# Moving layer 0's image resize and the weight preparation of layers 0 and 1 to the head of a four-layer convolution kernel

## The chip, the cores and the metric

The kernel runs on one core of a Trainium2 chip. A core has five instruction streams that run side by side and wait for one another through semaphores: TensorE (PE, with its weight loads shown apart as PEld), VectorE (DVE), ScalarE (ACT), GpSimd (POOL) and SyncE (SP), which here issues transfers only. Each stream runs its instructions in order. The metric is the device time of one execution, in microseconds.

## The reference

The input x has the shape (2, 64, 256, 256) in float32. Four layers follow, each of the form x = x + f(norm(x)), where norm is a group norm with 32 groups of two channels. A group norm needs the sums over the whole of x before the first element can be normalised.

```python
# layer 0
rimg = jax.image.resize(img, (b, 3, 256, 256), method='bilinear')    # from 512 x 512
rimg = jnp.einsum('oc,bchw->bohw', w_img, rimg)
em = jnp.concatenate([rimg, pos_embd], axis=1)        # pos_embd: w_pos times sines and cosines
feature_score = jnp.einsum('bckhw,bchw->bkhw', unfold3x3(em), em)    # dilation 2
comp_score = jax.nn.sigmoid(jnp.einsum('bckhw,c->bkhw', unfold3x3(inp), w_comp))
out = jnp.einsum('bckhw,bkhw->bchw', unfold3x3(inp), comp_score * feature_score)
```

Layer 1 is two Mamba blocks (a projection, a causal convolution of four taps, a scan over 65536 positions with 16 states, an output projection), each with a layer norm. Layer 2 is a projection to 384 channels, a filter in the Fourier domain of 8 x 8 patches, a 3 x 3 depthwise convolution, a gate and a projection back. Layer 3 is a quantised 8 x 8 cosine transform.

## The kernel before

The two images of the batch and their 64 channels fill the 128 partitions, and the 65536 pixels lie along the free axis. Everything is float32. Each layer reads its input from DRAM, writes its output to DRAM (y0, y1, y2, then out), and gathers the statistics of its output on the way; at its end `group_norm` makes the scale and shift ("coeffs", the tiles gns and gnb) for the next layer.

The order at the head of the program is this. `input_stats` (line 194) loads x in 16 tiles of 4096 columns (xin, three buffers) through SP, and DVE runs one bn_stats over each 512 columns, 128 in all (line 203). `group_norm` (bn_aggr at line 159, two small matmuls, a power on POOL at line 175, gnb at line 177) makes the coefficients.

`layer0` then calls `resize`. It loads the resize matrix rt and, for each of six images, loads src (line 218), multiplies it by rt in 32 matmuls (line 223), copies the four results from PSUM on ACT (mid, line 226), multiplies again in 16 matmuls (line 231), copies two results on DVE (dst, line 234) and stores them to the scratch tensor rimg in DRAM (line 235). src, mid, dst and the PSUM tile rps have two buffers each. After that `layer0` loads its own weights (pos, w_comp, w_e, w_y), makes wcomp and by_row, fills 32 partitions of the two tiles rts with the positions (line 274), and has POOL zero the frames gs and es and eleven tiles called moved (line 288). The memory of these tiles partly follows on that of `resize`.

Layer 0 itself is a pipeline of 128 steps of two image rows. A step normalises x (fea, line 191), makes the embedding e and the gated feature g (`embed`, lines 319 to 334), multiplies e by its shifted neighbours on POOL (pr, line 356), sums over channels on PE (pf, line 361), and puts the parts together (lines 366 to 440). Its order on every engine is written out by hand, between the lines `with tc.manual_schedule(...)`. Outside of such blocks a scheduler places the instructions of each engine: roughly in program order, but an instruction whose inputs are ready may be put ahead of one that must wait.

`layer1` first calls `mamba_weights` twice, for p1 and p2. Each call issues 26 small loads (helpers `load`, `load2` and `load_turned`, lines 134, 142 and 453, and lines 470 and 503) into temporary tiles, and rearranges them on DVE, ACT and PE into the kept tiles res, conv, dt, bc, a, d and out. The temporaries of p2 take the memory of those of p1. Ten further loads bring the layer norms' factors, sel and quad. Only then does `load(0)` (line 578) bring the first input tile x1t, and ACT normalises it into xin (line 191). The loop of layer 1 runs over 256 tasks (two blocks by 128 chunks of 512 positions), each in eight groups; its time is DVE's scan (line 792) and products.

All loads and stores of this kernel are issued by SP.

Of the kernel before, what the change touches and what calls it, by code (L numbers as in the profile page):

```python
# [10 lines left out]
F32 = mybir.dt.float32  # L11
# [3 lines left out]
PSUM = bass.MemoryType.PSUM  # L15
DRAM = bass.MemoryType.DRAM

P = 128
C = 64
# [101 lines left out]
class Kernel:  # L121
    def __init__(self, ctx, tc, a, out):
        self.tc, self.nc, self.a, self.out = tc, tc.nc, a, out
        self.const = ctx.enter_context(tc.tile_pool(name="const", bufs=1))
        self.dram = ctx.enter_context(tc.tile_pool(name="dram", bufs=1, space=DRAM))
        self.ident = self.load("c_ident")
        self.pair = self.load("c_pair")
        self.block = self.load("c_block")


    def load(self, name, pool=None):
        ap = self.a[name]
        t = (pool or self.const).tile(list(ap.shape), F32, name=f"t_{name}", tag=f"t_{name}")
        self.nc.sync.dma_start(t, ap)
        return t

    def load2(self, name, pool):

        ap = self.a[name]
        t = pool.tile([P, ap.shape[1]], F32, name=f"t_{name}", tag=f"t_{name}")  # L140
        for b in range(2):
            self.nc.sync.dma_start(t[b * C : (b + 1) * C], ap)
        return t

    def scratch(self, name, shape=(P, HW)):
# [45 lines left out]
        self.nc.scalar.activation(out, in_, AF.Identity, scale=coeffs[0], bias=coeffs[1])  # L191


    def input_stats(self, x):
        nc = self.nc
        stats = self.new_stats("stats_x")
        n = 4096
        with self.tc.tile_pool(name="in", bufs=3) as pool:
            for i in range(HW // n):
                t = pool.tile([P, n], F32, name="xin")  # L200
                nc.sync.dma_start(t, x[:, i * n : (i + 1) * n])
                for j in range(n // SUB):
                    nc.vector.bn_stats(
                        stats[:, i * (n // SUB) + j, :], t[:, j * SUB : (j + 1) * SUB]
                    )
        return self.group_norm("l0", stats, NSUB)


    def resize(self, rimg):
        nc, a = self.nc, self.a  # L210
        with self.tc.tile_pool(name="rs", bufs=2) as pool, self.tc.tile_pool(
            name="rsp", bufs=2, space=PSUM
        ) as psum:
            rt = pool.tile([P, 4, 256], F32, name="rt", bufs=1)
            nc.sync.dma_start(rt, a["c_resize"].rearrange("(k p) n -> p k n", p=P))
            for i in range(6):
                src = pool.tile([P, 4, 512], F32, name="src")
                nc.sync.dma_start(src, a["img"][i].rearrange("(k p) w -> p k w", p=P))
                mid = pool.tile([P, 4, 256], F32, name="mid")
                for wt in range(4):  # L220
                    ps = psum.tile([P, 256], F32, name="rps")
                    for k in range(4):
                        nc.tensor.matmul(
                            ps, src[:, k, wt * P : (wt + 1) * P], rt[:, k], start=k == 0, stop=k == 3
                        )
                    nc.scalar.copy(mid[:, wt], ps)
                dst = pool.tile([P, 2, 256], F32, name="dst")
                for ht in range(2):
                    ps = psum.tile([P, 256], F32, name="rps")
                    for k in range(4):  # L230
                        nc.tensor.matmul(
                            ps, mid[:, k, ht * P : (ht + 1) * P], rt[:, k], start=k == 0, stop=k == 3
                        )
                    nc.vector.tensor_copy(dst[:, ht], ps)
                nc.sync.dma_start(rimg[i].rearrange("(k p w) -> p k w", p=P, w=W), dst)

    def layer0(self, x, y, coeffs):

        nc, tc, a = self.nc, self.tc, self.a
        R = 8
        rimg = self.scratch("rimg", (6, HW))
        self.resize(rimg)
        stats = self.new_stats("stats_0")
        xv = x.rearrange("p (h w) -> p h w", w=W)
        yv = y.rearrange("p (h w) -> p h w", w=W)
        rv = rimg.rearrange("p (h w) -> p h w", w=W)
        nblk, per, nstep = H // R, R // 2, H // 2
        with ExitStack() as ctx:  # L250
            keep = ctx.enter_context(tc.tile_pool(name="l0k", bufs=1))
            pool = ctx.enter_context(tc.tile_pool(name="l0", bufs=2))

            pos = self.load("c_pos", keep)
            wc = self.load2("w_comp", keep)
# [3 lines left out]
            w_e = keep.tile([38, P], F32, name="w_e")  # L259
            w_y = keep.tile([32, P], F32, name="w_y")  # L260
            for t in (w_e, w_y):
                nc.vector.memset(t, 0.0)
            for b in range(2):
                nc.sync.dma_start(w_e[32 + 3 * b : 35 + 3 * b, C * b : C * b + 32], a["w_imgT"])
                nc.sync.dma_start(w_e[0:32, C * b + 32 : C * b + C], a["w_posT"][0:32])
                nc.sync.dma_start(w_y[:, C * b + 32 : C * b + C], a["w_posT"][32:64])
            by_row = keep.tile([P, H], F32, name="by_row")
            with tc.tile_pool(name="l0pr", bufs=1, space=PSUM) as psum:
                ps = psum.tile([P, H], F32, name="rowps")
# [109 lines left out]
            def add(eng, n, name, other):  # L379
                t = term[n, name]  # L380
                eng.tensor_add(t, t, other)

            load(0)
            load(1)
            E = mybir.EngineType
            with tc.manual_schedule(engines={E.PE, E.DVE, E.Activation, E.Pool, E.SP}):
                features(0)
                for t in range(nstep + 5):
# [6 lines left out]
                    n, last = t - 3, t - 4  # L395
# [21 lines left out]
                    if 0 <= n < nstep:  # L417
                        g, _, j = at(n)
# [16 lines left out]
                    if acc is not None:  # L435
                        k, s = divmod(last, per)
# [11 lines left out]
    def load_turned(self, name, pool):  # L448

        ap = self.a[name]  # L450
        t = pool.tile(list(ap.shape), F32, name=f"t_{name}", tag=f"t_{name}")
        for i in range(4):
            self.nc.sync.dma_start(t[i::4], ap[32 * i : 32 * i + 32])
        return t

    def mamba_weights(self, m, keep):
        nc, a = self.nc, self.a
        w = {}
        with self.tc.tile_pool(name=f"mw{m}", bufs=1) as pool, self.tc.tile_pool(
            name=f"mwp{m}", bufs=1, space=PSUM  # L460
        ) as psum:

            def kept(name, shape, dt=F32):
                return keep.tile(shape, dt, name=f"{m}{name}", tag=f"{m}{name}")
# [5 lines left out]
            nc.sync.dma_start(taps, a[f"{m}conv_wT"].partition_broadcast(P))  # L470
            w["conv"] = kept("conv", [P, 4, P])

            def turned(t):
# [14 lines left out]
            ps = psum.tile([P, P], F32, name=f"{m}ps")  # L488
# [11 lines left out]
                nc.vector.tensor_copy(w["bc"][:, j::8], bc[:, 5 - j : DS : 4])  # L500
            alog = pool.tile([P, 4, 4], F32, name=f"{m}alog")
            for q in range(4):
                nc.sync.dma_start(
                    alog[32 * q : 32 * q + 32],
                    a[f"{m}Alog"].rearrange("(i d) (q j) -> q d i j", d=32, j=4)[q],
                )
# [17 lines left out]
    def softplus(self, out, in_, bias):  # L524
        self.nc.scalar.activation(out, in_, AF.Softplus, bias=bias)

    def layer1(self, x, y, coeffs):
        nc, tc, a = self.nc, self.tc, self.a
        T = SUB
        nch = HW // T  # L530
        stats = self.new_stats("stats_1")
        with ExitStack() as ctx:
            keep = ctx.enter_context(tc.tile_pool(name="l1k", bufs=1))
            ws = [self.mamba_weights(m, keep) for m in ("p1_", "p2_")]
            mean = keep.tile([P, P], F32, name="mean")
            nc.scalar.mul(mean, self.block, 1.0 / C)
            lns = [(self.load2(f"ln{i}_g", keep), self.load2(f"ln{i}_b", keep)) for i in (1, 2)]
            sel = self.load("c_sel", keep).rearrange("k (b j p) -> k b j p", b=2, p=P)
            quad = self.load("c_quad", keep)
            eps = keep.tile([P, 1], F32, name="eps")  # L540
            nc.vector.memset(eps, 1e-5)
# [193 lines left out]
            with tc.manual_schedule(engines={E.PE, E.DVE, E.Activation, E.Pool, E.SP}):  # L735
# [29 lines left out]
                for g, (n, b, j) in enumerate(groups):  # L765
# [4 lines left out]
                    t, m = ts[n], tasks[n][0]  # L770
# [504 lines left out]
                nc.sync.dma_start(yv[:, rows], yt)  # L1275

    def run(self):
        x = self.a["x"]
        coeffs = self.input_stats(x)
        layers = (self.layer0, self.layer1, self.layer2, self.layer3)  # L1280
        for i, layer in enumerate(layers):
            y = self.out if i == 3 else self.scratch(f"y{i}")
            coeffs = layer(x, y, coeffs)
            x = y


@with_exitstack
# [52 lines left out]
```

## Time and profile before

| what | value |
|---|---|
| median of 3 runs | 19426.9 us (19423.29 to 19428.31) |
| the profiled execution | 19425.37 us |
| its span, first to last instruction | 19423.1 us |
| mean granted TensorE clock | 0.756 of full speed |
| DVE busy in the span | 17991.3 us, 93% |
| POOL busy | 16845.3 us, 87% |
| PE busy | 14534.9 us, 75% |
| ACT busy | 12151.6 us, 63% |
| costliest group | DVE scan, line 792, 8192 of 1262 ns |
| waits of SP's queue in `input_stats` for DVE | 58.9 us in 13 waits, longest 4.8 |

A row of the timeline gives the start in us, the time in us (of the whole group, where several like instructions are merged), the engine, the line, the operation with the tile it writes and those it reads, and in brackets the idle time before it and what ended it. SPq rows are the issuing of transfers, not the transfers themselves. The windows give the busy time of each engine within a stretch, and beside it the share of time in which the 16 DMA engines were at work.

### The profile page before, as it was taken

What the parts mean: (1) busy time and instruction counts of PE and PEld (TensorE: products, weight loads), DVE (VectorE), ACT (ScalarE), POOL (GpSimd) and SP (SyncE); (2) the same over time, 40 slices, a digit from 0 to 9 for tenths busy, and PEclk for the clock granted to TensorE, in tenths of its full rate; (3) what the DMA queues carried; (4) which work ended last, traced back from release to release, by engine and by line L of the source; (5) the groups of instructions that cost most, each with busy time, mean ns of one, the idle gap of its engine ahead of it and who ended that gap; (6) DMA issues with size and microseconds to landing.
All of it is one profiled execution on the core that took longest, in us unless ns stands there. A gap on an engine that the chain in (4) does not pass through costs nothing. (4 is left out here: it accounts for less than half of the span.)

```text
span 19423.1 us, 164029 instructions
## 1 busy us (share of the span) xinstructions
PE 14534.9 (75%) x48720; PEld 4763.2 (25%) x48720; DVE 17991.3 (93%) x15870; ACT 12151.6 (63%) x17418; POOL 16845.3 (87%) x8646
## 2 busy tenths in 40 slices
PE   7996677767777677676677677767777679999996
PEld 3441111111111111111111111111111134444444
DVE  6888999999999999999999999999999978888896
ACT  2325666666666666666666666666666657777774
POOL 5997888888888888888888888888888878888885
PEclk9996666666666666667666666666666679999997
DMA  3116666666666666666666666666666621111104
GB/s 122 57 50 150 149 156 152 150 155 149 155 150 151 156 151 152 150 150 155 152 151 154 149 156 150 150 156 151 152 150 151 154 52 32 32 32 31 32 29 147
DMA packets 662191, 2438.92 MB, mean 126 GB/s; under 512 B 131888, under 2 KB 201264, under 8 KB 450160
## 3 DMA queue, kind: packets, MB, share of 16 engines
q1 hardware_dynamic: 661296, 2428.43, 52.1%
q8 instruction: 385, 6.31, 0.1%
q14 instruction: 510, 4.18, 0.1%
HBM read 1990.14 MB, written 437.78 MB: 125 GB/s over the span
## 5 line engine op out<-in xcount | busy, mean ns | idle before, releaser
L792 DVE TENSOR_TENSOR_SCAN h<-da,st,h 128x512 f32<-128x512 f32 x8192 | 9837.9, 1262 | 310.0 <-ACT da L789 225.5
L796 POOL TENSOR_TENSOR h<-h,cb 128x2048 f32<-128x2048 f32 x2048 | 9252.4, 4518 | 164.7 <-POOL st L795 0.2
L789 ACT ACTIVATE da<-dl,p_a 128x512 f32<-128x512 f32 x8192 | 5564.3, 688 | 3976.2 <-DVE h L792 3884.3
L561 PE MATMUL py<-h,t_c_quad 128*32 128x512 f32 x16384 | 3250.7, 817 | 1649.2 <-POOL h L796 1648.3
L561 PE MATMUL pb<-bc,t_c_sel 64*128 64x512 f32 x3072 | 2696.1, 972 | 2386.6 <-DVE h L773 2381.3
L773 DVE TENSOR_TENSOR h<-dv,pb 128x2048 f32<-128x2048 f32 x1536 | 3471.5, 2260 | 40.8 <-DMA dv<-d_dv 40.8
L1023 POOL TENSOR_TENSOR gl<-gl,prod 128x512 f32<-128x512 f32 x2056 | 2606.1, 1272 | 460.9 <-ACT prod L1019 346.7
L755 POOL TENSOR_TENSOR h<-dv,cb 128x2048 f32<-128x2048 f32 x512 | 2318.7, 4529 | 16.7 <-DMA dl<-d_dl 16.7
L982 DVE SCALAR_TENSOR_TENSOR acc<-z,tap_b,acc 128x1024 f32<-128x1024 f32 (+1 forms) x1496 | 1901.6, 1271 | 22.3
L561 PEld LDWEIGHTS pb<-bc,t_c_sel 64*128 64x128 f32 x3072 | 660.9, 267 | 4410.5 <-DVE h L773 4347.0
L1019 ACT ACTIVATE prod<-z,tap_a 128x512 f32<-128x512 f32 x2056 | 1422.3, 716 | 284.8 <-POOL gl L1023 273.8
L795 POOL COPY st<-h 128x4 f32<-128x4 f32 x2048 | 383.5, 187 | 1362.9 <-DVE h L792 1331.9
L1079 PE MATMUL pcv<-z,diag 128*128 128x512 f32 x2322 | 1236.4, 642 | 179.9 <-ACT gl L1087 166.0
L561 PEld LDWEIGHTS py<-h,t_c_quad 128*32 128x32 f32 x16384 | 423.2, 122 | 3814.4 <-POOL h L796 3222.6
L561 PE MATMUL mm<-xin,p_conv 64*128 64x512 f32 x4096 | 1318.7, 773 | 15.1 <-DMA x1t<-y 15.1
L943 PE MATMUL pz<-t_c_inv,gf 128*128 128x128 f32 (+1 forms) x8192 | 964.7, 293 | 7.6 <-ACT z L951 7.3
L561 PE MATMUL mm<-u,p_dt 128*128 128x512 f32 x1024 | 929.1, 1061 | 0.0
L943 PEld LDWEIGHTS pz<-t_c_inv,gf 128*128 128x128 f32 (+1 forms) x8192 | 792.8, 170 | 484.2 <-issue 302.5
L924 DVE TENSOR_TENSOR gf<-feff,f 128x384 f32<-128x384 f32 x1024 | 558.7, 547 | 299.9 <-PE f L915 297.4
L561 PE MATMUL py<-u,p_d 128*128 128x512 f32 x1024 | 820.9, 895 | 0.0
L951 ACT COPY z<-pz 128x512 f32<-128x512 f32 x768 | 449.7, 590 | 411.1 <-PE pz L943 330.4
L561 PEld LDWEIGHTS mm<-xin,p_conv 64*128 64x128 f32 x4096 | 459.5, 244 | 980.8 <-issue 980.6
(169 smaller groups left out, 17244.8 us busy)
## 6 DMA issues: line engine op xcount, KB each, us to landing
cb<-d_bc SPq DMA_DIRECT2D x2048, 320.0 KB
dl<-d_dl SPq DMA_DIRECT2D x2048, 256.0 KB
dv<-d_dv SPq DMA_DIRECT2D x2048, 256.0 KB
d_dl<-delta SPq DMA_DIRECT2D x256, 512.0 KB
d_dv<-du SPq DMA_DIRECT2D x256, 512.0 KB
xin<-in_x SPq DMA_DIRECT2D x16, 2048.0 KB
xt<-in_x SPq DMA_DIRECT2D x32, 1024.0 KB
y<-yt SPq DMA_DIRECT2D x128, 256.0 KB
```

The source lines that it names most:

```text
L561: nc.tensor.matmul(out, lhsT, rhs, start=start, stop=stop)
L755: nc.gpsimd.tensor_tensor(h, t["dv", b], t["cb", b][:, 0].unsqueeze(1).to_broadcast([P, 4, T]), ALU.mult,)
L773: nc.vector.tensor_tensor(h, t["dv", b], pb.unsqueeze(1).to_broadcast([P, 4, T]), ALU.mult)
L789: nc.scalar.activation(da, t["dl", b][:, k], AF.Exp, scale=ws[m]["a"][:, k, j : j + 1])
L792: nc.vector.tensor_tensor_scan(h[:, k], da, h[:, k], state[m, b][:, j, k : k + 1], ALU.mult, ALU.add)
L796: nc.gpsimd.tensor_tensor(h, h, t["cb", b][:, 1 + j].unsqueeze(1).to_broadcast([P, 4, T]), ALU.mult)
L924: nc.vector.tensor_tensor(o, feff, ph[b], ALU.mult)
L943: nc.tensor.matmul(pz[i * n : (i + 1) * n, k, :, 16 * g : 16 * g + 16], gf[t, 2 * e + g, b][:, c0 : c0 + n], inv, start=True, stop=True,)
L982: eng.scalar_tensor_tensor(out, near(s, name, m0, r, k), w, box["t"], ALU.mult, ALU.add)
L1019: nc.scalar.activation(prod, near(s, name, 4 * h + m, n, k), AF.Copy, scale=w)
L1023: nc.gpsimd.tensor_add(acc, acc, prod)
L1079: nc.tensor.matmul(box["t"], diag[:, k], near(s, f"a{i}", 4 * h + m, n, k), start=k == 0, stop=k == 8,)
```

## The change

Three things move and one queue is changed.

- `layer1_weights`, a new function, holds what stood at the head of `layer1`, and `run` calls it first of all. Its kept tiles live through layers 0 and 1.
- `layer0` makes its weights, rts and frames first and then calls `input_stats`. The copies that fill rts go from DVE to POOL.
- The six images are resized inside `input_stats`: the third, seventh, eleventh tile of x and so on is followed by an image. x comes in 32 tiles of 2048 columns with five buffers, and both PSUM copies of the resize are on ACT. rimg is stored through POOL's queue; src is still loaded through SP's.
- `self.queue` is ScalarE's queue until layer 1 begins and SP's from there on. All weight loads and the load of rt use it.

The three scratch tensors y0, y1 and y2 are made at the start. The loops of all four layers are the same as before.

```diff
+        self.queue = tc.nc.scalar
...
-        self.nc.sync.dma_start(t, ap)
+        self.queue.dma_start(t, ap)
...
-    def input_stats(self, x):
-        nc = self.nc
+    def input_stats(self, x, rimg):
+        nc, a = self.nc, self.a
         stats = self.new_stats("stats_x")
-        n = 4096
-        with self.tc.tile_pool(name="in", bufs=3) as pool:
+        n = 2048
+        with self.tc.tile_pool(name="in", bufs=5) as pool, self.tc.tile_pool(
+            name="rs", bufs=2
+        ) as images, self.tc.tile_pool(name="rsp", bufs=2, space=PSUM) as psum:
+            rt = images.tile([P, 4, 256], F32, name="rt", bufs=1)
+            self.queue.dma_start(rt, a["c_resize"].rearrange("(k p) n -> p k n", p=P))
+
+            def resize(i):
+                src = images.tile([P, 4, 512], F32, name="src")
+                nc.sync.dma_start(src, a["img"][i].rearrange("(k p) w -> p k w", p=P))
...
+                    nc.scalar.copy(dst[:, ht], ps)
+                nc.gpsimd.dma_start(rimg[i].rearrange("(k p w) -> p k w", p=P, w=W), dst)
...
+                if i % 4 == 2 and i // 4 < 6:
+                    resize(i // 4)
...
-    def layer0(self, x, y, coeffs):
+    def layer0(self, x, y):
...
-        self.resize(rimg)
-        stats = self.new_stats("stats_0")
...
-                nc.vector.tensor_copy(t[0:32], pos.unsqueeze(1).to_broadcast([32, R, W]))
+                nc.gpsimd.tensor_copy(t[0:32], pos.unsqueeze(1).to_broadcast([32, R, W]))
...
+            coeffs = self.input_stats(x, rimg)
+            stats = self.new_stats("stats_0")
+            pool = ctx.enter_context(tc.tile_pool(name="l0", bufs=2))
...
+    def layer1_weights(self, keep):
+        nc = self.nc
+        ws = [self.mamba_weights(m, keep) for m in ("p1_", "p2_")]
...
+        return ws, mean, lns, sel, quad, eps
+
+    def layer1(self, x, y, coeffs, weights):
...
     def run(self):
...
+        with ExitStack() as ctx:
+            keep = ctx.enter_context(self.tc.tile_pool(name="l1k", bufs=1))
+            weights = self.layer1_weights(keep)
+            y0, y1, y2 = (self.scratch(f"y{i}") for i in range(3))
+            coeffs = self.layer0(self.a["x"], y0)
+            self.queue = self.nc.sync
+            coeffs = self.layer1(y0, y1, coeffs, weights)
+        coeffs = self.layer2(y1, y2, coeffs)
+        self.layer3(y2, self.out, coeffs)
```

More of the change, by code (lines that the diff above doesn't have):

```diff
@@ L141, in load2 @@
         for b in range(2):
-            self.nc.sync.dma_start(t[b * C : (b + 1) * C], ap)
+            self.queue.dma_start(t[b * C : (b + 1) * C], ap)
         return t
@@ L191, in affine @@
         self.nc.scalar.activation(out, in_, AF.Identity, scale=coeffs[0], bias=coeffs[1])
-    def input_stats(self, x):
-        nc = self.nc
+    def input_stats(self, x, rimg):
+        nc, a = self.nc, self.a
         stats = self.new_stats("stats_x")
-        n = 4096
-        with self.tc.tile_pool(name="in", bufs=3) as pool:
+        n = 2048
[7 more added lines that the diff above has]
+                nc.sync.dma_start(src, a["img"][i].rearrange("(k p) w -> p k w", p=P))
+                mid = images.tile([P, 4, 256], F32, name="mid")
+                for wt in range(4):
+                    ps = psum.tile([P, 256], F32, name="rps")
+                    for k in range(4):
+                        nc.tensor.matmul(
+                            ps, src[:, k, wt * P : (wt + 1) * P], rt[:, k], start=k == 0, stop=k == 3
+                        )
+                    nc.scalar.copy(mid[:, wt], ps)
+                dst = images.tile([P, 2, 256], F32, name="dst")
+                for ht in range(2):
+                    ps = psum.tile([P, 256], F32, name="rps")
+                    for k in range(4):
+                        nc.tensor.matmul(
+                            ps, mid[:, k, ht * P : (ht + 1) * P], rt[:, k], start=k == 0, stop=k == 3
+                        )
+                    nc.scalar.copy(dst[:, ht], ps)
+                nc.gpsimd.dma_start(rimg[i].rearrange("(k p w) -> p k w", p=P, w=W), dst)
             for i in range(HW // n):
@@ L205, in input_stats @@
                     )
+                if i % 4 == 2 and i // 4 < 6:
+                    resize(i // 4)
         return self.group_norm("l0", stats, NSUB)
[L209 to L235, printed above, removed]
-    def layer0(self, x, y, coeffs):
+    def layer0(self, x, y):
         nc, tc, a = self.nc, self.tc, self.a
@@ L251, in layer0 @@
             keep = ctx.enter_context(tc.tile_pool(name="l0k", bufs=1))
-            pool = ctx.enter_context(tc.tile_pool(name="l0", bufs=2))
             pos = self.load("c_pos", keep)
@@ L263, in layer0 @@
             for b in range(2):
-                nc.sync.dma_start(w_e[32 + 3 * b : 35 + 3 * b, C * b : C * b + 32], a["w_imgT"])
-                nc.sync.dma_start(w_e[0:32, C * b + 32 : C * b + C], a["w_posT"][0:32])
-                nc.sync.dma_start(w_y[:, C * b + 32 : C * b + C], a["w_posT"][32:64])
+                self.queue.dma_start(w_e[32 + 3 * b : 35 + 3 * b, C * b : C * b + 32], a["w_imgT"])
+                self.queue.dma_start(w_e[0:32, C * b + 32 : C * b + C], a["w_posT"][0:32])
+                self.queue.dma_start(w_y[:, C * b + 32 : C * b + C], a["w_posT"][32:64])
             by_row = keep.tile([P, H], F32, name="by_row")
@@ L452, in load_turned @@
         for i in range(4):
-            self.nc.sync.dma_start(t[i::4], ap[32 * i : 32 * i + 32])
+            self.queue.dma_start(t[i::4], ap[32 * i : 32 * i + 32])
         return t
@@ L469, in mamba_weights @@
             taps = pool.tile([P, 4, P], F32, name=f"{m}taps")
-            nc.sync.dma_start(taps, a[f"{m}conv_wT"].partition_broadcast(P))
+            self.queue.dma_start(taps, a[f"{m}conv_wT"].partition_broadcast(P))
             w["conv"] = kept("conv", [P, 4, P])
@@ L502, in mamba_weights @@
             for q in range(4):
-                nc.sync.dma_start(
+                self.queue.dma_start(
                     alog[32 * q : 32 * q + 32],
@@ L525, in softplus @@
         self.nc.scalar.activation(out, in_, AF.Softplus, bias=bias)
-    def layer1(self, x, y, coeffs):
+    def layer1_weights(self, keep):
+        nc = self.nc
+        ws = [self.mamba_weights(m, keep) for m in ("p1_", "p2_")]
+        mean = keep.tile([P, P], F32, name="mean")
+        nc.scalar.mul(mean, self.block, 1.0 / C)
+        lns = [(self.load2(f"ln{i}_g", keep), self.load2(f"ln{i}_b", keep)) for i in (1, 2)]
+        sel = self.load("c_sel", keep).rearrange("k (b j p) -> k b j p", b=2, p=P)
+        quad = self.load("c_quad", keep)
+        eps = keep.tile([P, 1], F32, name="eps")
+        nc.vector.memset(eps, 1e-5)
+        return ws, mean, lns, sel, quad, eps
+    def layer1(self, x, y, coeffs, weights):
         nc, tc, a = self.nc, self.tc, self.a
@@ L532, in layer1 @@
         with ExitStack() as ctx:
[L533 to L541, printed above, removed]
+            ws, mean, lns, sel, quad, eps = weights
             io = ctx.enter_context(tc.tile_pool(name="l1io", bufs=3))
@@ L1277, in run @@
     def run(self):
[L1278 to L1284, printed above, removed]
+        with ExitStack() as ctx:
[7 more added lines that the diff above has]
+        self.layer3(y2, self.out, coeffs)
 @with_exitstack
```

## Prediction

> **What bounds it now.** I read the windows by stage first, then the timeline at the two seams that the change touches. The columns of the windows are: stretch, its length, busy us (and instructions) of PE, PEld, DVE, ACT and POOL, granted clock, DMA share, GB/s.
>
> ```profile
> core 0: us, PE busy (x) PEld busy (x) DVE busy (x) ACT busy (x) POOL busy (x), PEclk, DMA share, GB/s
> 10.00:40.00 30.00, 0.00 (x0) 0.00 (x0) 29.16 (x49) 0.00 (x0) 0.00 (x0) 1.00 1.01 429
> ...
> 95.00:171.00 76.00, 65.35 (x288) 56.77 (x288) 5.17 (x13) 11.02 (x26) 0.00 (x0) 1.00 0.32 111
> 171.00:204.00 33.00, 18.39 (x19) 4.99 (x20) 7.51 (x6) 8.49 (x17) 32.57 (x27) 0.50 0.02 5
> ...
> 1455.00:1498.00 43.00, 5.02 (x14) 2.75 (x12) 11.98 (x37) 2.86 (x8) 1.10 (x4) 0.57 0.15 32
> ```
>
> Four limits follow one another: the statistics (DVE and DMA both full), the resize (PE alone), the zeroing of frames (POOL alone), and, at 1455, the weights of layer 1 with nobody busy. The last three are serial and cheap to hide. The 14200 us of layer 1 (1515 to 15715) are none of the change's business: DVE is busy 93% of the span and nothing in layer 1's loop is edited. Next, the timeline of the first seam (start, us, engine, line, operation).
>
> ```profile
> 88.51 3.62 DVE L159 BATCH_NORM_AGGREGATE mv<-stats_x 128x2 f32<-128x768 f32 x1
> ...
> 95.12 0.81 ACT L191 ACTIVATE fea<-xt,gnb_l,gns_l 128x512 f32<-128x512 f32 x1 [7.68 <-DVE gnb_l L177]
> 95.15 0.38 SPq L215 DMA_DIRECT2D rt<-in_c_resize  x1
> ...
> 168.50 0.42 DVE L234 COPY dst<-rps 128x256 f32<-128x256 f32 x1 [1.30 <-PE rps L231]
> 171.32 0.35 SPq L134 DMA_DIRECT2D t_c_pos<-in_c_pos  x1
> ...
> 190.18 0.84 ACT L328 ACTIVATE e<-pe,by_row 128x256 f32<-128x256 f32 x2 [1.41 <-PE pe L321]
> 191.17 2.48 POOL L334 TENSOR_TENSOR g<-fea,sg 128x512 f32<-128x512 f32 x2
> ...
> 193.62 4.36 POOL L356 TENSOR_TENSOR pr<-e 128x512 f32<-128x512 f32 x4
> ```
>
> The coefficients exist at 95.1, yet layer 0's first products (pr) start at 193.62: 76 us of resize, then loads, then POOL's memsets. The second seam:
>
> ```profile
> 1460.02 3.60 DVE L159 BATCH_NORM_AGGREGATE mv<-stats 128x2 f32<-128x768 f32 x1
> ...
> 1466.48 0.16 DVE L177 SCALAR_TENSOR_TENSOR gnb_l<-mg,gns_l 128x1 f32<-128x1 f32 x1 [0.73 <-POOL gns_l L175]
> ...
> 1497.57 1.31 SPq L578 DMA_DIRECT2D x1t<-y  x3
> 1500.70 1.52 ACT L191 ACTIVATE xin<-x1t,gnb_l,gns_l 128x512 f32<-128x512 f32 x2 [7.69 <-DMA x1t<-y]
> ```
>
> Layer 1's coefficients exist at 1466.6. Its first input load stands on SP behind 62 weight loads, some 0.6 us each, and xin starts at 1500.70.
>
> **Second seam, the surer gain.** With the weights made long before, xin waits for coefficients and for x1t alone. The sums at 1460.02 were also held: DVE had a copy of a weight ahead of them that waited for its load until 1459.84, while the last statistics ended at 1458.78. So the coefficients come 1.2 us earlier, at 1465.4. The load x1t to xin took 3.1 us (1497.57 to 1500.70); SP is free after the last store of y, issued by 1459.7. If x1t must wait for that store to land, some 2 to 3 us (estimate, from the 3.1 of the load), it arrives at 1465 to 1466. Gain: 1500.70 - 1465.5 = 35 us, bounds 30 and 36. What follows on the path is the same chain.
>
> **First seam.** From coefficients to pr, with no memset in the way: fea 0.81, then the rows from pl (180.23) to the second e (191.02) 10.8, with PE at the same low clock: 11.7. So with the coefficients at C, pr starts at C + 11.7, and the gain is 181.9 - C. All depends on C, which was 95.1 and becomes later, since work is put into a stage that is full.
>
> - Bytes. x is 33.55 MB, 78.2 us at 429 GB/s. The images and the resize matrix add 6.82 MB, 15.9 us at that rate. The weights: 0.15 of 43 us, 6.5. The six stores of rimg: the window 95.2 to 171 has a share of 0.32, 24.3 DMA-us, less 15.9 leaves 8.4, of which five precede the end, 7.0. First tile: issued 2.12, used 9.71, less 4.9 for its 2.1 MB, 2.7 of latency. Last tile in: 2.1 + 2.7 + 78.2 + 15.9 = 98.9, or 112.4 with all the small transfers. Then four bn_stats (0.61 apart) 2.4 and the group norm 6.6: C is 108 to 121.
> - DVE alone: 9.7 + 78 + 6.6, plus some 7 of weight work (6.07 in 1466.6 to 1500.7, and by_row, wcomp), is 101. Under the DMA's sum, so not the end. The 12 dst copies go to ACT: 12 x 0.37 (the mid row, same shape) is 4.5 us there, beside idle time. PE's 65 us lie beside the statistics, in which PE does nothing; that cover gone is case D.
> - Here a rule speaks against the change. The Trainium skill's page DMA: Bandwidth & Descriptors, section Issuing engines are not separate DMA queues, says that DMAs of all issuing engines share the same 16 engines, and another queue saves only issue time. By the DVE row alone C would stay near 101 (first-seam gain 81); by the rule each byte adds its time, 108 to 121 (61 to 74). The row shows share 1.01 already, so I go with the rule: ACT's queue gives no bandwidth.
> - SP's order. Each image load stands on SP between x tiles and there are two src buffers. Image 2, behind x tile 10, waits until image 0 has gone through its first 32 matmuls. Those need rt, whose load is on ACT in program order after 3 constants, 62 weights and 9 loads of layer 0: 75 x 0.6 = 45 us (ACT's issue cost is not in the trace; SP's 0.6 is the nearest row; at 0.3, as for SP's short ones, 23). The psum of the resize may also follow by_row's. So image 0 leaves src at 45 + 9.7 = 55, and all 11 x tiles before are used up by about 43: DVE runs dry for 12 us. After 55, 21 tiles and 4 images of 1.05 MB: 25 x 2.44 = 61 us, + 2.7, + half of the stores 3, + 9.0: **C = 131**. Images then come every 12.2 us and PE needs 10.4 (116.50 to 126.86), so this waiting happens once.
> - Weights in two rounds: p2's temporaries reuse p1's memory. On a quiet DMA p2 took 14 us (1479.25 to 1493.3) and p1 about as much, within the 45. Beside the x stream, each small packet waits for large ones; at worst the weights are done only when SP has stopped: two rounds and the rest from 40 on, resize from 75, C = 152.
> - POOL: 20 us of memsets (171.4 to 191.2), two rt copies (2.7 to 4.1 on DVE; I take 4 each on POOL) and six store issues (price not shown; between 0 and the 2.5 of a g pair, I take 1) are 34 us against C's 131, when POOL otherwise does nothing. Cover gone, up to 34 us return. Behind the last store on POOL stands the group norm's power, and the coefficients wait for it; the store waits for image 5's copy. Image 5 comes with nine tiles left, 22 us, and takes 10.4 on PE: in time, with 10 us to spare. The Trainium skill's page SBUF — State Buffer, section SBUF: two separate sides, says that DVE's two-port copies keep GpSimd from writing its DMA's descriptors, which speaks against POOL stores. The row that shows such a lock is wcomp, 3.22 us beside a memset against 0.29 for a like operation at 1477.14; but bn_stats, nearly all of DVE's work here, takes 0.694 beside a busy POOL and 0.676 beside an idle one. By the rule at its worst six stores slip by 3 us each, 18 us, all but the last ahead of need; by the row, nothing. I take nothing.
>
> Sum: 181.9 - 131 = 51, plus 35: 86 us. From the profiled execution's 19425.4 (span 19423.1 and 2.3 around it): 19339. The median shown is 1.5 above that execution, which changes nothing here.
>
> **Rivals.**
> - A, no stall on SP: if rt and the weights come early (ACT issuing at 0.3 us, or rt put ahead of weights), C = 115, gain 67 + 35, 19323. For it: the program before has its loads placed out of program order (layer 1's st memsets run at 0.81). Against it: rt's load and psum stand last.
> - B, the forecast: 19339.
> - C, the weights trickle beside the x stream: C = 152, gain 30 + 33, 19362. For it: 3760 packets under 512 B in the weights' window, against x's rows (8 KB after the change) at share 1.01.
> - D, the work is moved but nothing is hidden: the statistics are queued on DVE behind all the weights and the resize, C above 178, and only the second seam remains, within 0.2% (39 us; about what a measurement of this kernel can tell from no change). Against it: DVE's resize copies are gone.
> - E, slower: layer 1 pays. The scratch tensors are made in another order, so the spill tiles lie elsewhere, and the transfers at a share of 0.66 land later. 2048 groups take 6.93 us each; 61 ns more per group (0.49 us per task of eight) would eat the 86 and 39 more. At 0.5 us on each of 256 tasks: 128 us, 19467. Against it: DVE waits only 40.8 us in all for dv.
>
> **Numbers.** B 0.45, A 0.23, C 0.18, D 0.07, E 0.07. The time is B's, 19339. A, B and C hold 0.86; with their ends, the DVE floor (gain 81 + 36, 19308) and C with 12 us more (19375), the range is 19308 to 19375. Faster is A, B, C: 0.86; same D, 0.07; slower E, 0.07.
>
> **What would show it.** bn_aggr of stats_x ends near 128 rather than 92.1, with one gap of some 12 us in bn_stats near 45, and SP waiting for PE rps at src. First pr at about 143. Memsets of g and e inside the statistics. xin about 4 us after the last store of y. Wrong if the first xin still waits for a load issued late, if src waits repeat for every image, or if layer 1's groups are not 6.93 us.

## The result, and the profile after

The changed kernel takes 19366.23 us (median of 7 runs, 19363.10 to 19368.11), against 19426.37 (7 runs, 19423.29 to 19428.31) before: a ratio of 0.9969, 95% interval 0.9958 to 0.9981, a gain of 60 us. The forecast was 19339, a gain of 86; the time lies in the range, 4 us from what rival C gave. The profiled execution took 19366.2, with a span of 19364.4. First the windows of the changed kernel (columns as in the prediction).

```profile
core 0: us, PE busy (x) PEld busy (x) DVE busy (x) ACT busy (x) POOL busy (x), PEclk, DMA share, GB/s
10.00:54.00 44.00, 1.55 (x4) 0.99 (x4) 22.12 (x54) 2.75 (x8) 0.07 (x1) 1.00 0.66 224
...
71.00:115.00 44.00, 44.00 (x194) 38.34 (x195) 26.43 (x44) 8.64 (x24) 7.24 (x14) 1.00 0.84 326
```

Before, the statistics ran at a DMA share of 1.01 and 429 GB/s. Now, from 10 to 54 us, the DMA engines stand idle a third of the time, DVE is busy for half of it, and PE does almost nothing: the resize has not begun. All that was moved beside the statistics was to fill gaps; it made new ones. The timeline of the changed kernel at the first seam:

```profile
53.93 6.20 POOL L286 MEMSET g<- 128x3640 f32 x2 [53.48 <-DVE p_out L522]
...
61.89 8.80 DVE L255 TENSOR_SCALAR wcomp<-t_c_block,t_w_comp 128x128 f32<-128x128 f32 x1 [2.98 <-DMA t_w_comp<-in_w_comp]
...
62.51 0.44 ACTq L203 DMA_DIRECT2D rt<-in_c_resize  x1
62.64 8.06 DVE L230 BATCH_NORM_STATS2 stats_x<-xin 128x6 f32<-128x512 f32 x6
...
67.32 3.38 DVE L269 COPY by_row<-rowps 128x256 f32<-128x256 f32 x1
...
70.83 9.52 PE L212 MATMUL rps<-rt,src 128*128 128x256 f32 x32 [3.55 <-DVE by_row L269]
...
147.06 3.62 DVE L160 BATCH_NORM_AGGREGATE mv<-stats_x 128x2 f32<-128x768 f32 x1
...
153.50 0.16 DVE L178 SCALAR_TENSOR_TENSOR gnb_l<-mg,gns_l 128x1 f32<-128x1 f32 x1 [0.75 <-POOL gns_l L176]
154.23 1.31 SPq L304 DMA_DIRECT2D xt<-in_x  x3
159.49 0.81 ACT L192 ACTIVATE fea<-xt,gnb_l,gns_l 128x512 f32<-128x512 f32 x1 [23.47 <-DMA xt<-in_x]
...
170.06 4.40 POOL L357 TENSOR_TENSOR pr<-e 128x512 f32<-128x512 f32 x4
```

The coefficients come at C = 153.7 (95.1 before, 131 forecast). The resize starts at 70.8 rather than 45, and xt is loaded only after the coefficients, 0.6 us behind them. The first products start at 170.06, 23.6 us earlier than before. And the second seam of the changed kernel:

```profile
1436.52 3.62 DVE L160 BATCH_NORM_AGGREGATE mv<-stats 128x2 f32<-128x768 f32 x1
...
1443.00 0.16 DVE L178 SCALAR_TENSOR_TENSOR gnb_l<-mg,gns_l 128x1 f32<-128x1 f32 x1 [0.73 <-POOL gns_l L176]
...
1443.31 1.27 SPq L582 DMA_DIRECT2D x1t<-y  x3
1446.28 1.52 ACT L192 ACTIVATE xin<-x1t,gnb_l,gns_l 128x512 f32<-128x512 f32 x2 [37.73 <-DMA x1t<-y]
```

The weights no longer stand there. But x1t, too, is issued just behind the coefficients. The gain along the run, from the same rows of both traces:

| at | before | after | gain so far |
|---|---|---|---|
| coefficients of layer 0 | 95.1 | 153.7 | -58.6 |
| first pr | 193.6 | 170.1 | 23.6 |
| first xin of layer 1 | 1500.7 | 1446.3 | 54.4 |
| sums of layer 1's statistics | 15719.2 | 15670.0 | 49.2 |
| first xn of layer 2 | 15738.4 | 15681.9 | 56.5 |
| end of the span | 19423.1 | 19364.4 | 58.7 |

Layer 1 took 5 us more of its 14220, and layer 2's first load, now issued 7.5 us after the sums instead of 15.0, gave 7 back. Most of what remains to be explained lies before 170 us.

### The profile page after: what moved, and what is told of

Its sections match the earlier page's. It is cut to its first block, busy times and chain, and to the rows that moved or that the text cites. A ratio compares the mean times of both kernels' runs of the same rounds, so it can differ in the third digit from the quotient of the medians.

```text
span 19364.4 us, 164058 instructions
## 1 busy us (share of the span) xinstructions
PE 14523.5 (75%) x48720; PEld 4761.5 (25%) x48720; DVE 17986.3 (93%) x15856; ACT 12157.4 (63%) x17429; POOL 16858.7 (87%) x8654
## 4 chain that ended last, share of the span: by engine, by line
DVE 45%; PE 23%; POOL 12%; issue 8%; ACT 7%; DMA 3%; SPq 1%; DVEq 0%; POOLq 0%; ACTq 0%
DVE h L796 27%; DVE h L777 13%; POOL h L800 6%; PE mm L565 6%; POOL gl L1027 4%; PE pf L362 3%; PE pb L565 3%; DVE acc L986 3%; PE py L565 2%; PE acc L406 2%; PE pcv L1083 2%; DMA cb<-d_bc 2%; ACT L793 2%; ACT prod L1023 2%; PE pz L947 1%
```

## The experiments

Each time is that of one execution, beside the kernel before on the same chip (19424 to 19426), except where an interval is given; the seven runs of the changed kernel lie 5 us apart, so a smaller difference says nothing. C is read from the profiled execution. The letters of theories belong to each expectation: S of the last ones is not S of the first. I began with this: SyncE, held by the images, is what makes C late.

**Images' loads on POOL's queue**, so that they can't hold x's tiles on SP.

```diff
-                nc.sync.dma_start(src, a["img"][i]...)
+                nc.gpsimd.dma_start(src, a["img"][i]...)
```

> The changed kernel with one line different: the six images are loaded through POOL's queue instead of SP's. Theory S (SP's queue holds x back: from 80 us on each image load stands between x tiles and waits for the resize of the image two before it, 33.7 us of waits of src for PE rps): with no image on SP, x comes as fast as DVE and DMA take it. 42 of the 128 bn_stats are done at 70.7 in the changed kernel; 86 more at 0.61 end at about 123, so the coefficients come near 130 instead of 153.7. The resize itself still ends where it did (last store of rimg at 136, landed at 143), so the first pr moves only to about 155 (from 170.1), and the time is about 19351. Theory B (the DMA engines are the bound, bytes beside bytes): the coefficients stay at 150 or later and the time at 19366. Theory W (DVE is held by its own weight work): bn_stats show the same gaps as before, same time.

19362.8: C = 148.8, only 5 us earlier. No image stood on SP, but now the images set the pace: the resize ran from 81.3, ten microseconds later than before (rt's load went out at 69.9 for 62.5), to 145.9, and the group norm's small matmul stood behind it on PE. Of the DMA issues in the first 160 us (KB each, median us from issue to landing), this kernel's

```profile
src<-in_img POOLq DMA_DIRECT2D x6, 1024.0 KB, 12.9
```

answers to the changed kernel's

```profile
src<-in_img SPq DMA_DIRECT2D x6, 1024.0 KB, 7.2
```

The longer landing is not the price of the queue: in the last run below, where SP issues the images into a stream as full as this one, they take 12.8. What this run points at is the late start of the resize more than the images' hold on SP.

**One half of the change each.** First the images beside the statistics, with layer 1's weights made where they were before, at the head of layer 1; then the weights beside the statistics, with the images resized after them by the function of before.

```diff
+            weights = self.layer1_weights(keep)
             coeffs = self.layer1(y0, y1, coeffs, weights)
```

> The changed kernel with the weights of layer 1 made at the head of layer 1 again, through SP's queue; everything of layer 0 stays at the head. Theory S: the resize started late (70.8) because ACT issued 62 weight loads, with waits, before the resize matrix. Without them ACT has 13 loads, the resize starts near 12 to 15, images keep pace with x, and the coefficients come at the DMA's sum, near 113 (108 to 121); first pr near 129 (170.1 in the changed kernel), gain 41. The second seam is lost again: xin 43 us after the last yt instead of 11, 32 us. Time about 19357. Theory B (image loads between x tiles hold the stream whatever the weights do): the coefficients stay above 140, time 19385 or more.

```diff
-                if i % 4 == 2 and i // 4 < 6:
-                    resize(i // 4)
+        self.resize(rimg)
```

> The changed kernel with the resize after the statistics again (with its own PSUM copies on ACT and DVE and its stores on SP, as before the change), the weights and the frames still at the head. Theory S: x is not held by images, only by DVE's weight work, which cost about 30 us of waits up to 62 us; coefficients near 125, the resize then takes its 73 us, first pr near 125 + 73 + 12 = 210 (193.6 before the change), so the first seam loses about 16 us and the second gains 32: 19410. Theory C (the weights are free beside x): coefficients near 105, first pr near 190, time 19391.

Images alone: 19366.0, C = 119.0, first pr at 134.7; what the first seam gained, the second lost (43.7 us again). Weights alone: 19412.1, C = 125.0. So the images cost C 24 us and the weights 30, and 24 + 30 nearly make the 58.6 (both runs keep layer 0's own weights and the frames at the head, so the two overlap somewhat). The window of the kernel with images alone shows what the weights took away:

```profile
10.00:54.00 44.00, 33.49 (x125) 27.76 (x126) 35.90 (x56) 6.81 (x16) 13.64 (x16) 0.92 1.02 409
```

A share of 1.02, and PE already at the images.

**Weights through SP's queue** instead of ScalarE's.

```diff
-        self.queue = tc.nc.scalar
+        self.queue = tc.nc.sync
```

> The changed kernel with all weight loads through SP's queue (one word changed). In SP's order they stand ahead of the first x tile. Theory S: x begins only when they are issued, near 50 us; the resize matrix is there too, so no image waits; from there x and the images take the DMA's 94 us and more, coefficients near 157, time about 19369, as good as the changed kernel's: what ACT's queue wins for x at the front is lost again to the waits of the image loads. Theory Q (ScalarE's queue is what makes the overlap): coefficients 25 us later or more, time 19390 or more.

19372.0, C = 158.4: ScalarE's queue is worth 6 us of the time and 5 of C. The weights hardly flow beside x on it; nearly as much is lost as when they stand in one queue.

**The group norm's small tiles in memory of their own.** In the changed kernel SP held xt back for the last step that reads these temporaries (9.1 us of waiting for gnb_l).

```diff
-            mv = pool.tile([P, 2], F32, name="mv")
+            mv = self.const.tile([P, 2], F32, name="mv_{}".format(name), tag="gn_mv")
...
```

> The changed kernel with the group norm's six small tiles kept in the constant pool instead of a pool of their own. In the changed kernel xt was issued at 154.2, right after the coefficients (gnb at 153.5), because its memory is that of the small tiles; fea waited for it until 159.5. Theory X (the small tiles hold the first load of each layer): xt and x1t are issued before the coefficients, first pr 4.7 us nearer to them (11.7 after instead of 16.4), xin at 1443 less 4.7 (3.1 less than the coefficients-plus-load of now), and some 4 us in layer 2; time about 19354. Theory Y (the memory of the x and image tiles holds xt just as long): gain under 2 us, time 19365.

19348.1, better than expected. From this kernel's timeline:

```profile
146.55 1.31 SPq L304 DMA_DIRECT2D xt<-in_x  x3
...
152.60 0.16 DVE L178 SCALAR_TENSOR_TENSOR gnb_l<-mg_l,gns_l 128x1 f32<-128x1 f32 x1 [0.75 <-POOL gns_l L176]
```

xt is issued ahead of the coefficients (152.8), and pr starts at C + 10.7 rather than C + 16.4; x1t is issued ten microseconds before layer 1's coefficients, and the second seam falls from 11.3 to 8.4 us between the last yt and xin. Layer 3's group norm gains too: 10.9 us at its coefficients have become 18.1 at the end.

**wcomp on ScalarE**, away from the operation that took 8.80 us on DVE.

```diff
-            nc.vector.tensor_scalar(wcomp, self.block, wc, None, ALU.mult)
+            nc.scalar.activation(wcomp, self.block, AF.Copy, scale=wc)
```

> The changed kernel with wcomp made on ACT instead of DVE. Theory P (wcomp waits on DVE for POOL's run of memsets and copies: 8.8 us at 61.9 in the changed kernel, 0.29 for a like operation with POOL idle): the 8.8 us on DVE go, by_row comes earlier, the resize starts at the landing of its matrix, near 67 instead of 70.8, and all that follows moves by 4 us: coefficients near 150, time 19362. Theory N (other waits stand behind it): by_row and the resize start where they did, time 19366.

A miss: 19374.9, slower than the changed kernel. wcomp took 0.40 us there and DVE was not held, but the first image started later. From the timeline of this kernel:

```profile
77.18 8.92 PE L212 MATMUL rps<-rt,src 128*128 128x256 f32 x32 [8.26 <-DVE stats_x L230]
```

6.4 us later than in the changed kernel, and C came 5.7 later. The row names a bn_stats, but by_row was there at 69.4 and the last wait of PE was for rt. rt's load counts its semaphore up in 16 parts as it lands. In the changed kernel all of them came within 4.0 us of its issue. Here, by the trace's record of that semaphore, 14 came by 68.3 us and the last at 77.05, 14.8 us after the issue, and PE's wait for them ended at 77.07. The changed kernel's held DVE freed no x tiles, so the eighth of a run of x loads went out only at 71.1; here the eight were out by 65.7. That this backlog of x delayed the last part of rt fits, but is not shown.

**Weights' steps after the tile loop** (at the end of `input_stats`), and this with the two before it.

```diff
+            weights = self.layer1_weights(l1keep)
         return self.group_norm("l0", stats, NSUB), weights
```

> The changed kernel with the weights of layer 1 still at the head, but behind layer 0's loads, the resize matrix and the images in program order (four x buffers instead of five, for the memory). Theory M (what the weights cost is mostly the late start of the resize): the resize starts near 19, as without the weights (18.7), images keep pace, coefficients near 128 (119.0 without the weights, and 6.5 of DMA time, and a few us of DVE), first pr near 144, xin 11 us after the last yt; time about 19340. Theory L (DVE's waits for weight loads cost their 30 us wherever the weights stand): coefficients near 149, time 19361.

> The three edits together: group norm tiles in the constant pool, wcomp on ACT, layer 1's weights behind layer 0's loads. Theory M with X and P: 19340 less 12 less 3, 19325; coefficients near 125, first pr near 137. Theory L: 19346.

19361.1 and 19343.2; the 18 us between them are what the tiles apart gave alone, and C is the same (143.2 and 143.3). The first didn't do what it meant: the scheduler put the weights' steps back among the statistics (the first at 6.2 us). What it changed was that rt went ahead, the resize began at 19.9, and C was 143.2. So it tells nothing of DVE's waits. To move steps, an order had to be laid down, which the next two do. (Both of these, the next two and the last run have four x buffers instead of five, to make room.)

**DVE freed.** Layer 1's weights only loaded early, into tiles of their own; the steps queued on DVE behind the group norm's last (with its tiles apart, as above). In the second, rt and layer 0's small loads also stand ahead of the weights.

```diff
+            self.load_layer1(*pools)
...
+            with tc.issue_after(self.normed.ins):
+                weights = self.layer1_weights(l1keep)
```

> Layer 1's weights are only loaded ahead of the statistics, into memory of their own; what VectorE makes of them (all but two copies) is queued behind the last step of the group norm, where it sat idle for 29.3 us. The group norm's small tiles lie apart, as in the run with 19348.1. Theory V (VectorE, in order, waiting for the weights' loads between the statistics is what cost 30 us): the coefficients come at 126 to 132 us in place of 152.6, the first products some 11 us later, and the kernel takes about 19324. Rival D (the weights' transfers beside x's stream, or ScalarE's 75 issues ahead of the images' matrix, cost it): the coefficients stay past 145 us and the kernel takes 19340 or more.

> As the run before it, with the loads of layer 0's small weights and the images' matrix ahead of layer 1's on ScalarE's queue. If the late start of the resize (70.8 us) is the other half of the loss, the first image starts before 30 us, the coefficients come at about 120 to 124 us and the kernel takes about 19318. If it doesn't matter once VectorE is free, the time is that of the run before it within 3 us.

19372.9 with C = 161.6, and 19353.9 (5 runs, 19349.7 to 19356.7; ratio 0.9964, interval 0.9949 to 0.9978) with C = 142.2. (pr came 21 us after C in both, since xt waited 14 us for p_out, one of the steps put behind.) The order of the loads alone moved the start of the resize from 75.5 to 20.6 and C by 19.4 us. Theory V fell: with the steps gone, DVE was idle for 60.1 us waiting for x (17 times). The rival's number held, and SP's waits in the first 75 us of the first of the two (line, what was waited for, us in total, times, longest) show where:

```profile
SPq L234 <- DMA t_ln_g<-in_ln_g: 9.3, 2, 7.5
SPq L234 <- DMA t_w_comp<-in_w_comp: 8.7, 1, 8.7
SPq L234 <- DMA t_p_in_wT<-in_p_in_wT: 7.2, 1, 7.2
SPq L234 <- DMA t_p_xproj_bcT<-in_p_xproj_bcT: 5.8, 1, 5.8
SPq L213 <- DMA t_p_conv_b<-in_p_conv_b: 5.6, 1, 5.6
```

SP, which issues x, waits for weights to land, whose memory has nothing to do with x's. The same view of the changed kernel has it too:

```profile
SPq L228 <- DMA t_ln_b<-in_ln_b: 14.4, 2, 8.5
...
SPq L228 <- DMA t_p_D<-in_p_D: 7.9, 2, 7.2
...
SPq L228 <- DMA t_p_xproj_bcT<-in_p_xproj_bcT: 5.8, 1, 5.8
SPq L207 <- DMA t_p_dt_b<-in_p_dt_b: 5.0, 1, 5.0
...
SPq L228 <- DMA t_p_dt_b<-in_p_dt_b: 4.8, 1, 4.8
SPq L228 <- DMA w_e<-in_w_imgT: 3.2, 1, 3.2
SPq L207 <- DMA t_p_dt_wT<-in_p_dt_wT: 1.8, 1, 1.8
```

Together 42.9 of 75 us. Why is in the compiled program. Three of SP's first loads and three of ACT's, counted from 0 on each engine, with what each waits for, from the changed kernel:

```
2 L228 DMACopy xin<-in_x 128x2048 [waits DMAHW7_49]
3 L207 DMACopy src<-in_img 128x4x512 [waits DMAHW6_49]
4 L228 DMACopy xin<-in_x 128x2048 [waits DMAHW5_49]
...
6 L454 DMACopy t_p_conv_b<-in_p_conv_b 32x1 [waits DMAHW0_49]
7 L454 DMACopy t_p_conv_b<-in_p_conv_b 32x1 [waits DMAHW1_49]
...
12 L454 DMACopy t_p_dt_b<-in_p_dt_b 32x1 [waits DMAHW6_49]
```

The loads of SP and ACT take turns at eight semaphores, DMAHW0 to DMAHW7; it is the program that hands them out so. Each load waits until the one that last had its semaphore has landed. POOL's loads have eight others (DMASW0 to 7). The traces carry the semaphores' numbers and agree: eight for SP and ACT together, and eight more for POOL's loads in the run below.

One link of the chain: a tile of x went out at 21.0, the weight t_p_D (0.1 KB) at 22.3. The tile had landed at 28.3, the weight at 28.5. The tile that was to use the weight's semaphore next had been held for 7.2 us and went out at 28.5. So a small load beside x's stream lands late (a median of 4.1 us for t_p_dt_b and 5.5 for t_p_D, where the run with the weights late, on a quiet DMA, has 1.9 and 2.0), and the next tile waits for it.

**Semaphores freed.** First in the changed kernel, alone; then with DVE freed, rt ahead, and the tiles of the weights' making clear of xt.

```diff
+            self.queue = self.nc.gpsimd
             weights = self.layer1_weights(keep)
+            self.queue = self.nc.scalar
```

> The changed kernel, with only the loads of layer 1's weights issued by GpSimd, through its own queue; everything else stays, VectorE's steps and their waits between the statistics too. In the program of the changed kernel the hardware queues' loads share eight semaphores, whichever engine issues them: a load of x waits until the load that used its semaphore before it has landed, often a weight, which in turn waited for a tile of x. GpSimd's queue has eight of its own. Theory S (shared semaphores hold x's stream): SyncE's waits for the landing of weights, 43 us before 75 us in the changed kernel, all but go, the DMA share from 10 to 54 us rises from 0.66 to 0.85 or more, the coefficients come at 120 to 140 us in place of 153.7 and the kernel takes 19333 to 19352. Rival D (the small transfers themselves cost the stream its rate): the share stays under 0.75, the coefficients past 148 us, and the time within 6 us of 19366.

> As the run with the images' matrix first, with two changes: layer 1's weights are loaded through GpSimd's queue, and the two small tiles of their making lie beside the loads, so that the memory of layer 0's x tile hangs on none of VectorE's steps. Theory S: x and images flow as in the run without layer 1's weights (coefficients at 119.0 us), so the coefficients come at 117 to 124 us, the first products 11 us later, and the kernel takes about 19316, from 19348.1 of the run with the group norm's tiles apart less the 33 us between its first products and these. Rival D: coefficients at 140 us or later, 19337 or more.

Alone: 19366.3, C = 156.2, no gain, as the rival said, though not for its reason. SP's waits for layer 1's weights were gone from that view, rt went out at 2.2, and the share rose, to 0.76 instead of the 0.85 hoped for. But DVE, with the weights' steps still among the statistics, now held x back: SP waited 44.6 us for its bn_stats and 17.9 for by_row, for which the resize too waited until 69.1. wcomp, beside POOL's copies and memsets, took longer than ever. From this kernel's windows and timeline:

```profile
10.00:54.00 44.00, 2.71 (x6) 1.49 (x6) 26.66 (x61) 1.58 (x7) 34.12 (x55) 1.00 0.76 273
...
49.74 19.20 DVE L255 TENSOR_SCALAR wcomp<-t_c_block,t_w_comp 128x128 f32<-128x128 f32 x1 [4.16 <-DMA t_w_comp<-in_w_comp]
```

Both together: **19331.2 us** (4 runs, 19328.5 to 19332.3, against 19423.9 of 7 runs; ratio 0.9952, interval 0.9935 to 0.9968), the fastest of all. Its window:

```profile
10.00:54.00 44.00, 29.89 (x106) 24.27 (x107) 32.63 (x50) 4.58 (x15) 33.61 (x54) 0.92 1.02 391
```

The share is 1.02 again, SP's waits for the landing of weights are 5.5 us in all (49.7 in the run with the images' matrix first), and C = 132.5, pr at 143.2, xin at 1416.2. The expected 117 to 124 was missed. One wait stands out in the timeline of the same kernel:

```profile
69.82 0.52 DVE L515 COPY p_dt<-p_ps 128x128 f32<-128x128 f32 x2 [13.92 <-PE p_ps L513]
```

A small copy that I had put on POOL stood behind its 62 issues, a matmul behind the copy, and DVE behind the matmul. Without these 13.9 us C would be near 119, an estimate that takes the whole wait as lost. It may be too low: over nearly the same time ACT waited 12.1 us, until 65.1, for the weight p_alog, with two copies of the resize behind it. That was not tried.

## Why the prediction was right, and where not

**Right:** faster, by both seams; the second the surer; no stage of layer 1 that pays (5 us in 14220, where rival E needed 128); and the whole as 181.9 - C, so that a late C tells at once what it costs. SP's waiting for rps at src is there. The gap in bn_stats is not one of 12 us but nine waits for x, 23.4 us in all before 155, and xin came 10 us after the last store of y, not 4.

**The term that was mis-sized is C**: 131 in the sum, 153.7 measured. In the sum's own steps, image 0 leaves src at 55; it left at 80.4. From there to C the sum has 76 us; it took 73. The 25 us are the late start, 70.8 for 45. ScalarE's 75 issues did cost 0.6 each; but 12.4 us of waits for landings (10.7 for weights and constants, 1.7 for a tile of x) and 5.9 for DVE's p_mo stood between them, and rt went out at 62.5. It had landed at 66.6, but by_row, for which PE waited too, was done only at 70.7. The sum took two queues as two streams that share only the engines. They share eight semaphores as well, so SP meanwhile waited 42.9 us for weights.

**Two holds over the same time.** With all weights still early, five runs had rt out before 10 us. With both DVE's steps and the shared semaphores left, C was 143.2 and 143.3; with DVE freed alone 142.2; with the semaphores freed alone 156.2; with both freed 132.5, and the DMA full. So neither shows in an experiment of its own, but with the other gone the semaphores are worth 9.7 us and DVE's steps up to 24. (The last pair is not clean: the run with the semaphores freed alone has five x buffers, and its wcomp fell among POOL's memsets.) Where rt stayed behind the weights, freeing DVE gained nothing either (161.6).

**"This waiting happens once" failed too**, and the prediction had named it as a sign of being wrong. The resize started at 70.8; SP's order as compiled had image 2 after 15 tiles instead of 11 and only two or three tiles between those that followed, so the wait came at four images, 33.7 us in all. The two partly cancelled: at the sum's 2.44 us each, the four tiles more that were in by then are 10 us less to load, so of the 73 us some 7 are these waits (an estimate from the sum's own prices).

**The rule weighed there** (the Trainium skill, DMA: Bandwidth & Descriptors, Issuing engines are not separate DMA queues) held, and gave a floor: by it C was 108 to 121, and the kernel without layer 1's weights came near (119.0; its own sum, less their 6.5, is at most 115). But it prices bytes. With the share at 0.66 the loss was in issuing, which neither the rule nor the row of the trace before (one queue, share 1.01) could show.

**Rival C** had the place and nearly the price (C = 152, 19362). Its cause, small packets waiting for large ones, is half of what was found: the weights did land late. But the engines had time; what cost it was that x's tiles waited for these landings.

**xt and x1t.** C + 11.7 became C + 16.4, and the second seam's 35 became 32: both loads waited for coefficients, because of the memory that they were given. I had reasoned about queues and never asked whose memory a first load takes over. With that undone it was C + 10.7.

**POOL.** The memsets were hidden, as said. "I take nothing" for the lock was wrong for one operation: wcomp took 8.80 us, against 3.22 before. That is not 8.80 us of DVE's time: the six bn_stats behind it started 0.6 us apart as ever and are on record as ending with it, at 70.7, as is by_row. But until then nothing was freed, and SP waited 4.8 us for by_row. Taking wcomp off DVE didn't help, since rt then landed later. Outside of this stretch bn_stats and the stores showed no such price.

**Not foreseen:** 7 us at layer 2's start, where the compiled order put loads elsewhere, 2 more in layers 2 and 3, and 5 lost in layer 1. That the time lies in the range owes something to luck: without these 9.5 us it would be 19375.7, just past the range's end of 19375.

## What to carry to other kernels

A second issuing queue is free only if its loads hold nothing in common with the first: look for waits of the one for landings of the other, since a set of semaphores that both use in turn makes a large stream wait for many small loads. Before work is moved into a full stage, sum what each engine will wait for in order, and not only what it will do. When an experiment that removes a suspected wait gains nothing, look what ends last then; two holds over the same time have to be removed together.

## What the runs showed of the hardware

- One DVE operation, tensor_scalar from SBUF to SBUF (128x128), took 0.40 us on ScalarE, 1.54 on DVE beside two copies of POOL's, 8.80 in the changed kernel and 19.20 when POOL was busiest. In the last case it ended at 68.94, when POOL's run of 17 memsets and copies since 47.65 had ended (68.85); in the changed kernel at 70.69, just after a memset of e (70.61), while POOL went on with the next. The Trainium skill's page SBUF — State Buffer, SBUF: two separate sides, says that of a GpSimd operation and a DVE one that needs the shared port pair, whichever starts first holds the pair for its whole instruction and the other fully blocks; here the block outlasted many of POOL's instructions. What lets DVE in at last isn't shown.
- The same images of 1 MB, beside x's stream, landed a median of 7.2 us after issue in the changed kernel. They took 12.9 from POOL's queue and 12.8 from SP's in two kernels whose streams ran at a share of 1.01 (71 to 115 us) and 1.02 (10 to 54); the changed kernel's had 0.84 (71 to 115). The fullness of the stream, not the queue, goes with the difference.
- Weights of 0.1 to 4 KB took a median of 2.3 to 6.7 us from issue to landing beside x's stream on ScalarE's queue, and those of them that a quiet DMA shows (0.1 to 2 KB) 1.9 to 2.3 there. One 512 KB load landed 4.0 us after its issue in one kernel and 14.8 in another, there with its last two of 16 parts 3 and 9 us behind the rest.
